# A decoder layer on one Trainium2 core: the first pass's single blocks become a pair, and the remainder block moves

## The chip, the cores and the metric

The kernel runs on one core of a Trainium2 chip. Five engines have queues of their own and work through them in order: TensorE (PE in the profile; its weight loads are shown as PEld), VectorE (DVE), ScalarE (ACT), GpSimd (POOL) and SyncE (SP), which here only issues transfers. ACT and POOL issue transfers too. 16 DMA engines move the data. The metric is the time of one execution in microseconds, the median of several runs. Everything is float32.

## The reference

One decoder layer of 16 sequences of 128 tokens and 1024 channels: self-attention, a cross-attention to a context, and a gated feed-forward layer whose weights are four-bit numbers with a scale and a zero for each group of 64.

```python
x = x + attn(layernorm(x), Wqkv, bqkv, Wo, bo)
x = x + xattn(layernorm(x), ctx, ctx, ...)
h = silu(xn @ Wg.T) * (xn @ Wu.T)
x = x + h @ Wd.T
```

Here `xn` is the normalised `x`; `Wg` and `Wu` are 2752 x 1024, `Wd` is 1024 x 2752, and each is computed from its packed numbers as `(w - zero) * scale`.

## The kernel before

**Stages.** Self-attention, cross-attention, the gate and up products of the feed-forward layer in two passes over the tokens (8 sequences each: first sequences 8 to 15, then 0 to 7), and the down products. All matrix products of the feed-forward layer are made in the manner of Strassen: seven products of half-sized operands take the place of eight, for some additions on other engines.

**Blocks.** The 2752 rows of `Wg` and `Wu` are cut into ten blocks of 256 and a remainder of 192 (`BLOCKS`, `RB = 10`). Two ways lead through them:

- `one_block` treats a single block by one level: for gate and for up seven products (`GATE`), each of four matrix multiplications with 512 columns of tokens (the tile is `p`). Each multiplication stands as two records in the profile, so a block has 112.
- `two_levels` treats pairs of blocks by two levels: seven outer products (`DOWN`, numbered 1, 2, 6, 5, 3, 7, 4), each of seven inner ones (1, 7, 6, 2, 5, 4, 3), each of four multiplications with 256 columns (the tile is `q`), 392 records a pair. GpSimd makes four left operands for each outer product (`li`, `inner_left`) from two tiles of weights (`w`), VectorE makes four right operands (`ti`, `inner_right`) in the pass's first pair. In the first pass these are stored in DRAM and loaded again for the later pairs (`again`); in the second, five of seven are kept (`KEPT`). VectorE also adds up the results (`got`, tiles `C`, `U`, `V`) and multiplies gate with up (`finish`, tile `h`).
- `last_block` treats the remainder by one level, 88 records of `p`.

The first pass takes blocks 0 and 1 one by one, then the pairs 1 to 4 (`PAIRS`, blocks 2 to 9), then the remainder. The second pass takes five pairs, then the remainder.

**Order around the change.** An engine wrapped in `InOrder` keeps the order of the program among its instructions; instructions issued without it (`nc.tensor` in block 0, `nc.gpsimd`) may be put elsewhere by the compiler. Cross-attention runs by `later(n, step)` and `tick()`: a step is run n ticks after it was noted. For each sequence VectorE and POOL divide four query tiles by their sums (`query_unit`, tile `qe`), VectorE turns them, they go out to DRAM and come back (`kd<-kt`, `qs<-kd`), and `project_out` then has four pieces (`mm<-qs,m_sb`), norms (`mm<-sq,ones`), and five steps up to `turned` and `turn_rows`, which writes the normalised rows to DRAM (`xt<-kt`). When the products of the feed-forward layer begin, the steps of the last three sequences are still to be done. They go beside block 0 and the beginning of block 1: `one_block` calls `between` after each of its 14 products, which is `beside` (L1644), and that makes one tick. From there on `moves` and `route` issue on POOL (L1133). When no step is left, `attention_done` (L1121) frees the memory of cross-attention, starts the next preparation of weights (`rest`) and opens the second set of PSUM banks.

**Preparation of weights.** `prepare` (L221) unpacks the four-bit weights on VectorE (`pa`, `pc`), stores them in DRAM (`wprep`) and is run in steps (`yield`) beside other work. The list `todo` (L324) is cut in three: `EARLY` jobs beside self-attention, those up to `MIDDLE` (18) beside cross-attention and block 0, the rest, with the first `LATE` (4) blocks of `Wd`, beside block 1 and the pairs of the first pass. The other seven blocks of `Wd` are prepared beside the second pass (`downs`, L1711). `between` in `two_levels` says how many steps go with an outer product.

**Loads of weights.** `to_load` is the list of weight tiles in order of use, `load_weights` issues the next one on SP, four tiles ahead (`AHEAD`); there are five buffers.

**Between the passes.** After the first pass's pairs, `new_blocks` and `block_loads` load the second pass's tokens (L1693 to L1697, four tiles of 1 MB, tile `b`, eight transfers). The first pass's remainder is multiplied meanwhile, and `outer_operand` forms three of four further operands from them beside it (L1662); the fourth is formed in the second pass's first pair (`last_operand`, L1479).

Of the kernel before, what the change touches and what calls it, by code (L numbers as in the profile page):

```python
# [3 lines left out]

# [78 lines left out]
def decoder_layer(  # L83
# [241 lines left out]
    EARLY, MIDDLE = 12, 18  # L325
    LATE = 4
# [265 lines left out]
    def block_loads(p, blocks, queue=nc.sync):  # L592

        for n, half in ((0, 0), (1, 0), (1, 1), (0, 1)):
            for i in range(2):
                src = xt_all[p][ds(half * BPT + 2 * i, 2), :, :, :, n]
                tc.keep_in_program_order(
                    queue.dma_start(
                        blocks[n, half][:, ts(i, TOKENS // 2)],
                        src.rearrange("b a c i j t -> (c i) (b a) j t"),  # L600
                    )
                )
                yield
# [55 lines left out]
    prep_pools(sides, "x", 2, 1)  # L659
# [18 lines left out]
    if True:  # L678
# [315 lines left out]
        for k, b in enumerate(batches):  # L994
# [15 lines left out]
            for n in (5,) if k < 12 else ():  # L1010
                later(n, lambda: next(middle, None))
# [99 lines left out]
    with ExitStack() as gs:  # L1111
# [9 lines left out]
        def attention_done():  # L1121

            nonlocal rest
            for _ in middle:
                pass
            sides.close()
            prep_pools(second, "f", 2, 2)
            rest = prepare(todo[MIDDLE:], 2, route, vector, route, loads_first=True)
            next(rest)
            banks.append(pool("c_u", 4, space=PSUM, side="right"))  # L1130
# [3 lines left out]
        flagged = []  # L1134
# [4 lines left out]
        SEQUENCE = [(mat, q) for mat in "gu" for q in GATE]  # L1139
        LAST = [("r", n) for n in range(2)] + [("m", q) for q in GATE]  # L1140

        def tiles_of(blk):
            todo = [(blk, *k) for k in (SEQUENCE if blk < RB else LAST)]
# [6 lines left out]
        PAIRS = [1, 2, 3, 4]  # L1150
        order = [blk for blk in range(RB) if blk // 2 not in PAIRS]
        order.insert(2 * PAIRS[0], None)
        to_load = deque([t for blk in order[: 2 * PAIRS[0]] for t in tiles_of(blk)])
        to_load += [t for i in PAIRS for t in tiles_of_pair(i)]
        to_load += [t for blk in order[2 * PAIRS[0] + 1 :] + [RB] for t in tiles_of(blk)]
        to_load += [t for i in range(NI) for t in tiles_of_pair(i)] + tiles_of(RB)
# [41 lines left out]
        def outer_operand(T, q):  # L1198

            b12 = blocks[0, 1]  # L1200
            if q == 7:
                vector.tensor_tensor(b12, T[3], b12, ALU.subtract)
                T[7] = b12
                return
            pool, tag = {5: (cxb, "b4"), 6: (xres, "X2"), 4: (xres, "X0")}[q]
            t = T[q] = pool.tile([P, TOKENS, JC, Q], F32, name=f"T{q}", tag=tag)
            a, b = {5: (b12, T[1]), 6: (T[3], T.get(5)), 4: (T[2], T.get(6))}[q]
# [42 lines left out]
        def one_block(blk, T, between):  # L1250

            sg = {}

            def gate(k, bank, add):
                t = sg[k] = ct.tile([P, TB], F32, name="sg", tag="sg")
                if add is None:
                    nc.scalar.activation(t, bank, AF.Silu)
                else:
                    vector.tensor_tensor(t, bank, add, ALU.add)
                    nc.scalar.activation(t, t, AF.Silu)  # L1260

            def up(k, bank, add):
                t = ch.tile([P, TB], F32, name="h", tag="h")
                if add is None:
                    vector.tensor_tensor(t, bank, sg[k], ALU.mult)
                else:
                    vector.tensor_tensor(t, bank, add, ALU.add)
                    vector.tensor_tensor(t, t, sg[k], ALU.mult)
                n, half = k
                store(blk, 1 + n, half, t)  # L1270


            engine = nc.tensor if blk == 0 else tensor
            make = {"g": products(T, gate, engine), "u": products(T, up, engine)}
            for n, (mat, q) in enumerate(SEQUENCE):
                make[mat](q)
                between(n, mat, q)

        def last_block(ps, T, between):


            PS = ps
            keys = {0: (1, 2), 1: ("e", 4)}[ps]
# [21 lines left out]
            def half_product(p, w, q, start, stop):  # L1305
                for j in range(JC):
                    tensor.matmul(
# [17 lines left out]
            between(0, "r", 0)  # L1325
# [4 lines left out]
            put_stores()  # L1330
            half_product(0, ws[0], 5, False, False)
            between(1, "r", 1)
            half_product(0, ws[1], 3, False, True)
            small(1, bank[0], bank[0])

# [24 lines left out]
            make = products(T, got)  # L1360
            for n, q in enumerate(GATE):
                make(q)
                between(2 + n, "m", q)
# [4 lines left out]
        KEPT = {1: "X8", 6: "X10", 5: "X12", 4: "X14", 7: "X4"}  # L1368
# [3 lines left out]
        class Operands:  # L1372


            def __init__(self, T, kept):
                self.T, self.kept, self.R, self.pool = T, kept, {}, None
                self.stored = {}

# [9 lines left out]
            def new(self, q):  # L1388

                tag = self.kept.get(q, "ti")  # L1390
                pool = {"ti": self.pool, "X4": xres}.get(tag, xlate)
                self.R[q] = pool.tile(
                    [P, 4, HT // Q, CHUNKS, Q],
                    F32,
                    name="ti",
                    tag=tag,
                    bufs=1 if self.kept else 3,
                )
# [61 lines left out]
        def two_levels(ps, pairs, operands, steps, between):  # L1460

            scalar = InOrder(tc, nc.scalar)
            OUTERS = [(i, q) for i in pairs for q in DOWN]
            R, place = operands.R, operands.pool
# [14 lines left out]
            def last_operand():  # L1479
                outer_operand(operands.T, 4)  # L1480
                extra.extend(operands.inner_right(4))

# [4 lines left out]
            def multiply(n, p):  # L1487
# [3 lines left out]
                if set_ == p:  # L1491
                    bank[p] = banks[n % 2].tile([P, 2, HT], F32, name=f"q{p}", tag="gu")
# [70 lines left out]
            def prepare_outer(n):  # L1563
                state[n] = {"L": {}, "bank": {}, "kept": {}}

                where = (place, "li") if ps == 0 else (ch, "h") if n == 0 else (ct, "sg")
# [7 lines left out]
            for n, (i, q) in enumerate(OUTERS):  # L1574
                last = n + 1 == len(OUTERS)
                if q in (1, 5):
                    where, name = (xres, "X6") if (ps, q) == (1, 5) else (place, "U" if q == 1 else "V")
                    sums["U" if q == 1 else "V"] = where.tile(wide, F32, name="UV", tag=name)
                load_weights()
                if n + 2 < len(OUTERS) and i > pairs[0] - (q in (7, 4)):  # L1580
# [17 lines left out]
                if ps == 1 and n == 0:  # L1598
                    extra.append(last_operand)
# [34 lines left out]

        deep = ExitStack()
# [5 lines left out]
        T1 = {}  # L1641
        first_operands, second_operands = Operands(T, {}), Operands(T1, KEPT)

        def beside(n, mat, q):  # L1644
            if rest is None:
                tick()
                if plain and not flagged and n == 5:
                    flagged.append(raise_flag())
                if not pend:
                    attention_done()  # L1650
            if blk == 2 * PAIRS[0] - 1:
                if n == 7:
                    assert rest is not None
                    route.engine = nc.sync
                    first_operands.pool = deep.enter_context(
                        tc.tile_pool(name="c_d", bufs=1, reuse_waits="tile")
                    )
                    right.extend(first_operands.inner_right(DOWN[0]))
                if n in (7, 8, 9, 11):
                    right.popleft()()  # L1660

            if blk == RB:  # L1662
                for k in {("m", 7): (5,), ("m", 6): (7,), ("m", 2): (6,)}.get((mat, q), ()):
                    outer_operand(T1, k)
                if (mat, q) == ("m", 1):
                    for step in second_operands.inner_right(1):
                        step()

            if blk == 0 and n in (2, 4, 6, 8, 10, 12):
                next(middle, None)  # L1670
            if rest is None or blk == 0 or blk == 1 and n < 4:
                return
            if blk == RB:
                steps = n < 2
            else:
                steps = n in (4, 5, 8, 10, 12)
            for _ in range(steps):
                next(rest, None)

        right = deque()  # L1680
        for blk in order:
            if blk is None:
                route.fine = True
                two_levels(
                    0,
                    PAIRS,
                    first_operands,
                    rest,
                    lambda n, i, q: {1: 2, 2: 2, 5: 2, 7: 0}.get(q, 1) if i > PAIRS[0] else 0,
                )  # L1690
                route.fine = False
                deep.close()
                cxb = pool("c_xb", 1)  # L1693
                pass1 = new_blocks(cxb, lambda k: f"b{k}")
                for _ in block_loads(1, pass1):
                    pass
                T1.update({1: pass1[0, 0], 2: pass1[1, 0], 3: pass1[1, 1]})  # L1697
                continue
            one_block(blk, T, beside)
        blk = RB  # L1700
        blocks.update(pass1)
        last_block(0, T, beside)
# [296 lines left out]
```

## Time and profile before

| | us |
|---|---|
| median of 3 runs | 2182.37 (2182.31 to 2183.66) |
| the profiled execution | 2184.46 |
| its span, first to last instruction | 2182.7 |

The stages, from the busy times by stretch (start and end in us from the span's start):

| stage | from | to | length | PE busy | DVE busy | DMA share |
|---|---|---|---|---|---|---|
| self-attention | 0.00 | 250.40 | 250.40 | 240.19 | 211.15 | 0.54 |
| cross-attention | 250.40 | 750.62 | 500.22 | 499.81 | 392.44 | 0.71 |
| block 0, end of cross-attention | 750.62 | 814.85 | 64.23 | 64.23 | 47.90 | 0.89 |
| block 1 | 814.85 | 862.91 | 48.06 | 48.06 | 25.95 | 0.67 |
| first pass, four pairs | 862.91 | 1203.04 | 340.13 | 339.42 | 239.96 | 0.72 |
| first pass, remainder | 1203.04 | 1240.81 | 37.77 | 37.77 | 22.93 | 0.97 |
| second pass, five pairs | 1240.81 | 1664.15 | 423.34 | 423.34 | 314.99 | 0.59 |
| second pass, remainder | 1664.15 | 1712.88 | 48.73 | 48.39 | 14.18 | 0.87 |
| down products | 1712.88 | 2182.70 | 469.82 | 461.80 | 232.65 | 0.72 |

PE busy is the time in which a matrix multiplication was under way; since they overlap, their spacing, a stage's length by its count, is the better price. Many instructions are recorded at L79, the helper in `InOrder`, so groups are told apart by their tiles.

### The profile page before, as it was taken

The numbers are of one execution on the slowest core, as the hardware profiler recorded it, in microseconds if no ns is written. First come the engines' busy times: TensorE is split into PE (matmuls) and PEld (weight loads), VectorE is DVE, ScalarE is ACT, GpSimd is POOL, SyncE is SP. The second block draws the span as 40 slices with busy tenths as digits, with TensorE's granted clock in tenths as the row PEclk, the third lists the DMA queues.
The fourth block names the chain that finished last, engine by engine and source line by source line (L and its number), as shares of the span: only waits on it lengthen the run. The fifth ranks groups of instructions, "written<-read, shape, count | busy, mean of one in ns | idle before, by whom it ended". The sixth has DMA issues, their size and how long they took to land.

```text
span 2182.7 us, 25252 instructions
## 1 busy us (share of the span) xinstructions
PE 2163.0 (99%) x8836; PEld 1611.3 (74%) x8836; DVE 1502.1 (69%) x2057; ACT 521.2 (24%) x704; POOL 768.7 (35%) x673
## 2 busy tenths in 40 slices
PE   8999999999999999999999999999999999999998
PEld 7565655555555555888888588888886788888887
DVE  7899578888877774777677677767765535544473
ACT  2111235655665541121122112212111000000000
POOL 5454133333343352444444244444441022323200
PEclk9999999999999999999999999999999999999999
DMA  6436447777797686577785846566657578979941
GB/s 258 150 130 223 148 152 232 226 230 234 229 293 222 191 284 225 188 269 252 268 272 195 244 150 198 201 220 229 202 185 249 188 209 228 300 178 259 269 122 59
DMA packets 266471, 467.18 MB, mean 214 GB/s; under 512 B 29504, under 2 KB 123712, under 8 KB 261344
## 3 DMA queue, kind: packets, MB, share of 16 engines
q1 hardware_dynamic: 219296, 370.04, 52.4%
q0 software_dynamic: 29312, 77.35, 13.0%
q10 hardware_dynamic: 17728, 18.09, 2.6%
q8 instruction: 72, 1.18, 0.2%
q14 instruction: 63, 0.52, 0.1%
HBM read 307.30 MB, written 157.55 MB: 213 GB/s over the span
## 4 chain that ended last, share of the span: by engine, by line
PE 95%; DVE 3%; issue 1%; DMA 1%; ACT 0%; POOL 0%; DVEq 0%; POOLq 0%
PE q L79 34%; PE po L1878 21%; PE kq L79 10%; PE mm L79 8%; PE p L79 6%; PE kx L79 5%; PE mm L435 4%; PE p L1229 2%; PE mm L450 2%; PE mm L333 1%; DVE pa L79 1%; PE tr L382 1%; DVE ti L79 0%; DVE pc L79 0%; PE mm L465 0%
## 5 line engine op out<-in xcount | busy, mean ns | idle before, releaser
L79 PE MATMUL q<-ti,li 128*128 128x256 f32 x1512 | 347.6, 379 | 0.7 <-ACT k L79 0.6
L79 PEld LDWEIGHTS q<-ti,li 128*128 128x128 f32 x1512 | 286.8, 190 | 41.3 <-ACT k L79 1.5
L79 ACT COPY k<-q 128x512 f32<-128x512 f32 x189 | 110.6, 585 | 589.9 <-PE q L79 589.8
L79 POOL TENSOR_TENSOR li<-w 128x512 f32<-128x512 f32 x126 | 173.6, 1380 | 114.8 <-DMA w<-wu 66.3
L865 POOL TENSOR_TENSOR qe<-qe,qrec 128x1024 f32<-128x1024 f32 x64 | 148.4, 2318 | 179.5 <-DVE qrec L79 142.2
L1878 PE MATMUL po<-wc,lc 128*128 128x256 f32 x840 | 184.0, 379 | 0.3 <-DVE wc L79 0.2
L1878 PEld LDWEIGHTS po<-wc,lc 128*128 128x128 f32 x840 | 159.4, 190 | 22.8 <-DVE wc L79 1.1
L79 POOL TENSOR_TENSOR li<-w,li 128x512 f32<-128x512 f32 x63 | 90.5, 1437 | 230.3 <-PE q L79 203.0
L79 DVE TENSOR_TENSOR C<-q,k 128x512 f32<-128x512 f32 x135 | 92.5, 685 | 85.0 <-PE q L79 82.1
L79 PE MATMUL q<-b,w 128*128 128x256 f32 x576 | 136.1, 379 | 0.0
L79 POOL TENSOR_TENSOR li<-li,w 128x512 f32<-128x512 f32 x63 | 84.8, 1346 | 124.5 <-PE q L79 124.3
L1878 PE MATMUL po<-wq,lq 128*128 128x256 f32 x560 | 126.7, 379 | 0.0
L79 PEld LDWEIGHTS mm<-qs,m_sb 128*128 128x128 f32 x512 | 97.3, 190 | 39.7 <-issue 28.9
L79 DVE STREAM_TRANSPOSE kt<-qe 128x1024 f32<-128x1024 f32 x64 | 79.3, 1240 | 62.0 <-POOL qe L865 57.9
L79 PE MATMUL kx<-ek,cxt 128*128 128x512 f32 x256 | 121.8, 598 | 0.0
L79 PEld LDWEIGHTS q<-b,w 128*128 128x128 f32 x576 | 109.4, 190 | 15.7 <-issue 1.0
L79 PE MATMUL mm<-qs,m_sb 128*128 128x256 f32 x512 | 120.6, 379 | 0.0
L79 PE MATMUL kq<-wq_sb,xn 128*128 128x512 f32 x256 | 120.2, 593 | 0.4 <-ACT qe L853 0.4
L79 PE MATMUL kq<-wk_sb,cx 128*128 128x512 f32 x256 | 120.1, 592 | 0.0
L79 PE MATMUL q<-ti,w 128*128 128x256 f32 x504 | 119.1, 379 | 0.0
L1878 PEld LDWEIGHTS po<-wq,lq 128*128 128x128 f32 x560 | 106.0, 190 | 15.5 <-issue 0.8
L435 PE MATMUL mm<-xnT,wqkv_sb 128*128 128x512 f32 (+1 forms) x320 | 113.3, 510 | 0.0
(205 smaller groups left out, 3777.8 us busy)
## 6 DMA issues: line engine op xcount, KB each, us to landing
w<-wu SPq DMA_DIRECT2D x140, 256.0 KB, 3.2
lq<-h SPq DMA_DIRECT2D x140, 256.0 KB, 5.1
w<-wg SPq DMA_DIRECT2D x138, 256.0 KB, 2.8
kd<-kt SPq DMA_DIRECT2D x62, 512.0 KB, 3.4
qs<-kd SPq DMA_DIRECT2D x244, 128.0 KB, 3.1
ti<-r SPq DMA_DIRECT2D x29, 1024.0 KB, 7.9
h<-h SPq DMA_DIRECT2D x80, 256.0 KB, 2.6
wq<-wd SPq DMA_DIRECT2D x70, 256.0 KB, 6.6
```

What stands on the lines that cost most here:

```text
L79: return lambda *args, **kw: self._tc.keep_in_program_order(fn(*args, **kw))
L333: tensor.matmul(ps, oT[:, d, ts(b % BPT, S)], wo_d[d][:, ts(h, 512)], start=(d == 0), stop=(d == 1),)
L382: nc.tensor.transpose(tr[:, j, :], xn[:, ts(4 * h + j, P)], ident)
L435: nc.tensor.matmul(ps[:, tokens], wqkv_sb[:, f, c, :], xnT[:, c, tokens], start=(c == 0), stop=(c == CC - 1),)
L450: nc.tensor.matmul(ps, xnT[:, c, ts(i, S)], wqkv_sb[:, 4:6, c, :], start=(c == 0), stop=(c == CC - 1),)
L865: nc.gpsimd.tensor_tensor(qe, qe, rec.unsqueeze(2).to_broadcast(wide), ALU.mult)
L1229: tensor.matmul(ps, wt[:, j, :], T[q][:, :, j], start=(first == q and j == 0), stop=(q in (2, 3, 4) and j == JC - 1), skip_group_check=True,)
L1878: nc.tensor.matmul(bank[:, i, :], l[:, ts(i, S)], w,  start=(start and c == 0 and i % 2 == 0), stop=(stop and c == len(pairs) - 1), skip_g ...
```

## The change

The first pass takes all five pairs by two levels; `one_block` is gone. The remainder of the first pass comes first, beside the end of cross-attention: its `between` is now called 11 times (four half products, seven products), makes one tick in each of the first three and two in each later one, and its multiplications go to `nc.tensor`. The preparation of the remainder's weights (`r`, `m`) is moved up to the place after the early jobs; five jobs rather than six are in the middle part, all beside cross-attention, and `LATE` is 3, so that the second pass prepares eight blocks of `Wd`. The first pass's pairs take two steps of preparation with each outer product but one, from the second pair on; the second pass's take two with all but two.

The second pass's token tiles are loaded during the last pair of the first pass, into memory that is free by then, and its first right operands are made there. The further operands (`outer_operand`) are all formed in the second pass's first pair, one of them in a tile of its own. `KEPT` names other places. In `two_levels` the sets of banks alternate across the seam.

```diff
     todo = [(blk, mat) for blk in range(RB) for mat in "gu"] + [(RB, "r"), (RB, "m")]
-    EARLY, MIDDLE = 12, 18
-    LATE = 4
+    todo[12:12] = [todo.pop(-2), todo.pop(-1)]
+    EARLY, MIDDLE = 12, 17
+    LATE = 3
...
-            for n in (5,) if k < 12 else ():
+            for n in (5,) if k < 13 else ():
                 later(n, lambda: next(middle, None))
...
-        PAIRS = [1, 2, 3, 4]
...
+        to_load = deque(tiles_of(RB))
+        to_load += [t for _ in range(2) for i in range(NI) for t in tiles_of_pair(i)] + tiles_of(RB)
...
-            pool, tag = {5: (cxb, "b4"), 6: (xres, "X2"), 4: (xres, "X0")}[q]
+            pool, tag = {5: (cxb, "b0"), 7: (cxb, "b1"), 6: (cxb, "b2"), 4: (xres, "X4")}[q]
             t = T[q] = pool.tile([P, TOKENS, JC, Q], F32, name=f"T{q}", tag=tag)
...
         def last_block(ps, T, between):
...
+            engine = nc.tensor if ps == 0 else tensor
...
-        KEPT = {1: "X8", 6: "X10", 5: "X12", 4: "X14", 7: "X4"}
+        KEPT = {1: "X12", 6: "X14", 5: "X10", 4: "X8", 7: "b3"}
...
+        for _ in middle:
+            pass
+        prep_side.close()
...
+        def beside(n):
+            for _ in range(1 if n < 3 else 2):
                 tick()
+            if plain and n == 4:
+                raise_flag()
+            if n >= 7:
+                right.popleft()()
+
         last_block(0, T, beside)
+        attention_done()
...
+        def take_block(n):
+            where = {2: (xres, "X6"), 6: (xlate, "X8"), 3: (xres, "X2"), 7: (xres, "X0")}
+            pool, tag = where[n]
+            key = AGAIN[len(pass1)]
+            pass1[key] = pool.tile([P, TOKENS, JC, Q], F32, name=f"b{key[0]}{key[1]}", tag=tag)
+            for _ in range(2):
+                next(again_loads)
+
+        def second_pass(i, q):
+            if i < NI - 1:
+                return []
+            if q in (2, 6, 3, 7):
+                take_block(q)
+            if q == 2:
+                T1[1] = pass1[0, 0]
+            return second_operands.inner_right(1) if q == 3 else []
+
+        route.fine = True
+        for step in two_levels(
+            0,
+            first_operands,
+            rest,
+            lambda n, i, q: 0 if i == 0 or q == 7 or (i, q) == (NI - 1, 3) else 2,
+            second_pass,
+        ):
+            step()
...
+        def outer_operands(i, q):
+            todo = {1: (5, 6), 2: (7,), 5: (4,)}.get(q, ()) if i == 0 else ()
+            return [lambda k=k: outer_operand(T1, k) for k in todo]
+
         remaining = two_levels(
             1,
-            range(NI),
             second_operands,
             downs,
-            lambda n, i, q: {2: 2, 5: 2, 3: 2, 7: 0}.get(q, 1) if i > 0 else 0,
+            lambda n, i, q: {6: 1, 7: 0}.get(q, 2) if i > 0 else 0,
+            outer_operands,
         )
```

## The prediction

> **What bounds the kernel now.** I read the page's busy times first, then the chain that ended last, then busy times by stretch, then the timelines of PE and POOL at the end of cross-attention.
>
> ```profile
> PE 2163.0 (99%) x8836; PEld 1611.3 (74%) x8836; DVE 1502.1 (69%) x2057; ACT 521.2 (24%) x704; POOL 768.7 (35%) x673
> ...
> PE 95%; DVE 3%; issue 1%; DMA 1%; ACT 0%; POOL 0%; DVEq 0%; POOLq 0%
> ```
>
> TensorE has work in 99% of the span and is 95% of the chain. A change pays here by taking TensorE time away, and costs where TensorE has to wait. The chain from the first pass to the down projection (start, us, what) gives a price for every stage:
>
> ```profile
> 814.85 48.07 PE p L79 x112
> 862.91 56.99 PE q L79 x264
> ...
> 943.78 259.27 PE q L79 x1200
> 1203.04 37.77 PE p L79 x88
> 1240.81 423.34 PE q L79 x1960
> ```
>
> `p` are products of 512 columns: 112 records are one block by one level, 48.07 us or 429 ns each; 88 are the remainder, 37.77. `q` are products of 256 columns: the second pass's five pairs are 1960 records in 423.34, so 392 records and 84.67 us a pair. Busy time by pair (stretch, length, then PE, PEld, DVE, ACT, POOL busy, clock, DMA share, GB/s):
>
> ```profile
> 862.91:947.60 84.69, 83.98 (x387) 72.71 (x386) 61.23 (x79) 15.85 (x25) 36.72 (x27) 1.00 0.62 220
> 947.60:1032.30 84.70, 84.70 (x394) 74.56 (x393) 57.24 (x74) 16.72 (x26) 38.76 (x28) 1.00 0.76 254
> 1032.30:1117.00 84.70, 84.70 (x395) 74.54 (x394) 59.97 (x79) 16.71 (x26) 37.77 (x28) 1.00 0.80 268
> ...
> 1579.50:1664.15 84.65, 84.65 (x393) 74.31 (x392) 64.21 (x83) 16.62 (x26) 34.73 (x25) 1.00 0.57 181
> ```
>
> Only the first pair has a hole in PE (0.71 us); a pair with VectorE at 64.21 of 84.65 has none.
>
> **One pair in place of two single blocks.** Removed: 2 x 48.07 = 96.14. Added: 84.67. That is -11.47 us on the engine that sets the end, the only gain in the change.
>
> [...]
>
> **The remainder beside the end of cross-attention.** Its 37.77 us move and cost the same; the question is the cover. From 750.62 to 814.85 TensorE did block 0 (48.07) and 16.16 us of cross-attention's last products, and block 1 followed. Now 37.77 + 16.16 = 53.93, and at 804.55 the first pair must start. The delayed steps of cross-attention come one per product for three products and then two per product (before: always one). So the last batch's four output pieces (`mm` from `qs`) stand behind the fifth product, before: two behind the sixth, two behind the seventh. PE:
>
> ```profile
> 769.56 1.88 PE L79 MATMUL mm<-sq,ones 128*128 128x512 f32 x4
> 771.28 7.03 PE L1229 MATMUL p<-T,w 128*128 128x512 f32 x16
> 778.15 3.62 PE L79 MATMUL mm<-qs,m_sb 128*128 128x256 f32 x16
> 781.60 3.60 PE L1229 MATMUL p<-b,w 128*128 128x512 f32 x8
> 785.03 3.62 PE L79 MATMUL mm<-qs,m_sb 128*128 128x256 f32 x16
> ```
>
> and POOL, which issues the loads of `qs`:
>
> ```profile
> 771.02 3.86 POOL L68 DMA_DIRECT2D qs<-kd  x7 [0.68 <-DMA w<-wu]
> 776.20 0.55 POOL L68 DMA_DIRECT2D qs<-kd  x1 [1.31 <-DMA kd<-kt]
> 778.40 2.18 POOL L68 DMA_DIRECT2D xt<-kt  x4 [1.65 <-DMA qs<-kd]
> 780.58 2.19 POOL L68 DMA_DIRECT2D qs<-kd  x4
> ```
>
> The second query's tile lands 6.9 us after its issue, 772.70 + 6.9 = 779.6, for a piece at 779.9; the fourth's lands 3.7 after 782.21, at 785.9, for a piece at 786.8. Both were just in time. In the new order TensorE is at the pieces one product (3.43) or two (6.86) earlier: second 776.4, fourth 779.9. If the loads stay, it loses 779.6 - 776.4 = 3.2, then is at the fourth at 783.1 and loses 2.8: 6.0 in all. Nothing of the change moves these loads: VectorE's and POOL's work on the queries (one TENSOR_TENSOR of 1.9 us each and its transpose) and POOL's four `xt` issues are still ahead of them. The lower bound is 0: the remainder's products are no longer held in program order with the others, so they may be put ahead of the pieces. But then VectorE is late next. Its two tests of the sums, at 789.9 and 793.8 before, stand in its queue ahead of the small product that frees the remainder's first bank. TensorE wants that bank at the eighth product: 774.7 + 6.9 (pieces) + 1.9 (norms) + 2 x 3.43 = 790.4. Without the weight preparation that VectorE did between the tests (3.3 us), the second ends at 791.7 and the bank is free at 792.5 or later: some 2 us from the other side. I take 4.5, between 0 and 6.0 and nearer to the upper row, because the order of these products before is exactly the program's.
>
> The remainder's nine weight loads and ACT's two copies go with it, and are fewer than block 0's fourteen loads in the same place. The operands of the first pair come in time in this picture: weights are loaded four tiles ahead, and the four `li` ran at 846.76 to 851.9 for a start at 862.91; VectorE's four `ti` go beside the remainder's last four products. The first pair's own loss of 0.7 to 1.2 us stays, and may grow by up to 1 with VectorE's backlog: 0.5.
>
> **Preparation of weights.** One step more (3.3 us of VectorE) goes into cross-attention, where TensorE needs 31.2 us a batch: 0. The first pass then has 5 gate/up jobs and 3 down jobs beside four pairs. A gate/up job on VectorE is two units of 2 x 0.41 + 1.22 + 1.22 and four sums of 0.68, 9.2 us; a down job is two units of 2 x 0.41 + 0.68 + 0.68 + 1.22 and two sums, 8.2. Together 70.6, or 17.7 a pair; their loads and stores go on SP's queue as before, and weight loads of the products stand behind them. What a pair needs by itself (rows `C`, `UV`, `h` of the first pass, 180.0 us over four) is 45.0. 62.7 of 84.7 is below the 64.21 that cost nothing: 0. The second pass takes an eighth down job: 8.2 / 4 = 2 us a pair more, 66.3 of 84.65: 0, and up to 1 if VectorE is then late for a bank. Without the cover of TensorE's 84.67 us a pair, these would be 70.6 and 8.2 in full.
>
> **Second pass's blocks beside the last pair.** The same eight loads of 512 KB, which took SP from 1207.23 to 1219.17 to issue and 7.4 us (median) to land:
>
> ```profile
> 1207.23 11.94 SPq L598 DMA_DIRECT2D b<-xt  x8
> ```
>
> They are now on SP in four groups between the weight and `ti` loads. Their targets were freed at least one outer product before, so SP should not wait. In 1203.04 to 1240.81 the queues moved 271 GB/s at a share of 0.97, so 4.2 MB is 15 us of all engines: 0.18 of a pair, on top of 0.80 at most. Behind them on SP stand the weight loads, and for those waits POOL, then TensorE. Weights of outer product n + 2 are loaded during n, and POOL reads them at the start of n + 1, 84.67 / 7 = 12.1 us later; they land in 3.5. A lag under some 9 us is hidden: 0, at worst 4.
>
> [...]
>
> **The seam.** The second pass now follows the first pair by pair. TensorE's banks alternate on, the first left operands and right operands are made beside the last pair. Three large subtractions (2.29 each) move from the remainder into the first pair: 64.16 + 6.9 = 71.0 of 84.7 on VectorE, denser than any row; 0 to 1.4, I take 0.5.
>
> **Sum.** -11.47 + 4.5 + 0.5 + 0.5 = -6.0. The profiled run took 2184.46, its span 2182.7, the median of the runs is 2182.37, so the span is worth the median to 0.02%: 2182.4 - 6.0 = **2176.4** (forecast, chance 0.46).
>
> **Rivals.**
> 1. Clean gain (0.20): the remainder's products fill the waits, 0 to 1.5 lost: 2171.7. For: they may be reordered. Against: VectorE's queue above.
> 2. Late loads (0.16): at the last pair the queues are full, weights or blocks come late and 4 more are lost: 2180.4, no change. For: share 0.80 before anything is added. Against: `ti` landed in 8.4 us and no product waited.
> 3. Slower (0.16): POOL's tail holds the first pair. POOL is in order, and its last `xt` issues ended at 821.17 before. If they stay there and the `li` of the first pair are queued behind them, the first is ready at 821.17 + 1.27 = 822.4 instead of 806.3, when the second inner product wants it: 16.1 lost, 2182.4 - 11.5 + 16.1 + 1 = 2188.0. It decides from 15.8 us late on. Against: the steps now come at two per product.
> 4. The change doesn't do what it says (0.02): still 3528 `q` records; 2182.
>
> About 0.2% (4.4 us) can be told from no change. Below 2178.0 lie the forecast but for a small part, and rival 1: 0.65; within, rival 2 and that part: 0.19; slower 0.16. The range runs from rival 1 without any loss to rival 2 and the beginning of rival 3: 2171 to 2184. The forecast's own: 2173 to 2179.
>
> **What would show it.** 3920 `q` and 176 `p` records; the pairs at 84.7 in both passes; PE gaps ended by DMA at `mm<-qs` about 775 to 786 (forecast), by VectorE at the remainder's eighth product (rival 1), by POOL `li` at 806 (rival 3), by loads in the last pair (rival 2). A pair above 85.5 us anywhere would make the prediction wrong.

## The result, and the profile after

The changed kernel takes 2207.32 us (median of 4 runs, 2202.57 to 2215.16) against 2183.01 for the kernel before on the same chip: a ratio of 1.0115, 95% interval 1.0083 to 1.0146. It is 1.15% slower. The profiled run took 2205.05, its span 2203.2; before, the span was 2182.7.

The page first, busy times and then the shares of the chain that ended last:

```profile
PE 2158.6 (98%) x9004; PEld 1643.9 (75%) x9004; DVE 1549.4 (70%) x2094; ACT 524.0 (24%) x709; POOL 800.4 (36%) x675
...
PE 88%; DVE 6%; DMA 3%; issue 2%; POOL 1%; ACT 1%; SPq 0%; DVEq 0%; POOLq 0%; ACTq 0%
```

TensorE's busy time fell by 4.4 us while the span grew by 20.5, and its share of the chain fell from 95% to 88%. (The busy time fell by less than the forecast's 11.47 mostly because records at half clock, shown below, count as busy.) So TensorE waits. For whom, from the feed-forward layer's first product on (749 us; engine, line, what was waited for: us in total, times, longest; the longest five):

```profile
PE q L80 <- DVE ti L80: 9.8, 4, 3.4
PE p L1222 <- DVE h L80: 7.0, 1, 7.0
PE po L1836 <- DMA lq<-h: 2.6, 1, 2.6
PE q L80 <- ACT k L80: 2.5, 3, 1.4
PE mm L80 <- DMA qs<-kd: 1.4, 1, 1.4
```

The two largest are both VectorE: one wait of 7.0 in the remainder (`p`), four of 9.8 together for right operands (`ti`). Stage by stage, taken from the first TensorE record of each stage:

| stage | before or expected, us | after, us | lost, us |
|---|---|---|---|
| remainder beside the end of cross-attention | 53.93 | 66.64 | 12.7 |
| first pair of the first pass | 86.31 | 86.70 | 0.4 |
| pairs 2 to 4 of the first pass | 84.61 | 84.61, 84.61, 84.76 | 0.1 |
| last pair of the first pass | 84.61 | 87.05 | 2.4 |
| first pair of the second pass | 84.61 | 97.80 | 13.2 |
| its other four pairs | 84.68 (mean) | 84.70 (mean) | 0.1 |
| remainder, down projection, end | 518.68 | 523.07 | 4.4 |

With 1.3 won ahead of the first product this makes 32.0, against a gain of 11.47: +20.5, the difference of the spans. 3920 `q` and 176 `p` records show that the change does what it says.

**The head.** TensorE and VectorE of the changed kernel, in order (start, length, what, and in brackets the idle time before it and what ended it):

```profile
799.53 2.82 PE L1222 MATMUL p<-T,w 128*128 128x512 f32 x6
809.41 6.64 PE L1222 MATMUL p<-b,w 128*128 128x512 f32 x8 [7.05 <-DVE h L80]
```

and VectorE in the same stretch:

```profile
802.37 1.23 DVE L80 SCALAR_TENSOR_TENSOR y<-sq,y 128x1024 f32<-128x1024 f32 x1 [5.66 <-ACT sq L939]
803.63 1.28 DVE L80 SCALAR_TENSOR_TENSOR X<-y,gs_sb,X 128x1024 f32<-128x1024 f32 x1
...
807.99 0.16 DVE L80 SCALAR_TENSOR_TENSOR shift<-mv,rstd 128x1 f32<-128x1 f32 x1 [0.67 <-POOL rstd L153]
...
808.67 0.68 DVE L80 TENSOR_TENSOR h<-p,k 128x512 f32<-128x512 f32 x1
```

The remainder's last product needs a bank that `h<-p,k` empties. Its input was done at 802.35, but the addition stood in VectorE's queue behind the last sequence's steps: `y`, itself idle for 5.66 us until ScalarE's exponential was done, then `X`, the statistics and `shift`. It ran 6.3 us late, and TensorE stood still for 7.05. The eight products that follow take 6.64 us where a row of eight took 3.60 before.

**The seam.** The last pair of the first pass and the first two of the second (stretch, length, then PE, PEld, DVE, ACT, POOL busy, clock, DMA share, GB/s):

```profile
1156.55:1243.60 87.05, 85.17 (x393) 74.18 (x392) 71.95 (x86) 16.67 (x26) 42.67 (x30) 1.00 0.86 279
1243.60:1341.40 97.80, 87.49 (x394) 75.21 (x393) 78.24 (x88) 16.69 (x26) 36.28 (x27) 0.98 0.46 145
1341.40:1426.00 84.60, 84.60 (x393) 74.44 (x392) 62.00 (x84) 16.69 (x26) 40.99 (x28) 1.00 0.66 218
```

The same pair in the kernel before, the first of the second pass:

```profile
1240.81:1325.48 84.67, 84.67 (x394) 74.51 (x394) 64.15 (x80) 16.39 (x27) 36.84 (x27) 1.00 0.45 156
```

VectorE around the second of the waits:

```profile
1268.83 2.28 DVE L80 TENSOR_TENSOR T<-b,b 128x2048 f32<-128x2048 f32 x1
1271.03 0.68 DVE L80 TENSOR_TENSOR C<-q,k 128x512 f32<-128x512 f32 x1
1271.74 1.74 DVE L80 TENSOR_TENSOR C<-C,UV 128x512 f32<-128x512 f32 x1
1273.40 1.75 DVE L80 TENSOR_TENSOR ti<-T 128x512 f32<-128x512 f32 x1
1275.18 0.69 DVE L80 TENSOR_TENSOR ti<-T,ti 128x512 f32<-128x512 f32 x1
```

and TensorE there:

```profile
1271.36 1.89 PE L80 MATMUL q<-ti,li 128*128 128x256 f32 x8
1276.02 3.62 PE L80 MATMUL q<-ti,li 128*128 128x256 f32 x8 [2.78 <-DVE ti L80]
```

VectorE does 78.24 us of work in the second pass's first pair, against 62.00 in the next and 64.15 in the same pair before. It is in no pair full, yet TensorE waits: the `ti` that a product needs at 1273.2 comes fourth behind a subtraction of 2.28. Of the four waits (0.84, 2.78, 2.78 and 3.38 us) the first three stand behind such a subtraction; the last, at 1332.69, has none in its outer product, but right operands among VectorE's additions.

In the last pair of the first pass the longest wait, 1.4 us, is one for ScalarE's `k`, and it comes before any right operand is made there (1217 us). From the chain that ended last:

```profile
1178.96 1.68 DVE pa L80
1180.66 2.18 DVE pa L80
...
1184.45 1.77 DVE pc L80
...
1189.16 33.15 PE q L80 x152
```

These are steps of the preparation of weights. The sum `C` stands behind them on VectorE, ScalarE waits 2.61 us for `C`, and its copy of `k`, which TensorE needs, stands behind that.

### The profile page after: what moved, and what is told of

It reads as the page before. It is cut to its first block, busy times and chain, and to the rows that moved or that the text cites. A ratio compares the mean times of both kernels' runs of the same rounds, so it can differ in the third digit from the quotient of the medians.

```text
span 2203.2 us, 25710 instructions
## 1 busy us (share of the span) xinstructions
PE 2158.6 (98%) x9004; PEld 1643.9 (75%) x9004; DVE 1549.4 (70%) x2094; ACT 524.0 (24%) x709; POOL 800.4 (36%) x675
## 4 chain that ended last, share of the span: by engine, by line
PE 88%; DVE 6%; DMA 3%; issue 2%; POOL 1%; ACT 1%; SPq 0%; DVEq 0%; POOLq 0%; ACTq 0%
PE q L80 35%; PE po L1836 19%; PE kq L80 10%; PE mm L80 8%; PE kx L80 5%; PE mm L437 4%; PE mm L452 2%; DMA wq<-wd 2%; PE p L80 2%; PE mm L335 1%; DVE pa L80 1%; DVE C L80 1%; DVE ti L80 1%; PE p L1222 1%; PE p L1272 1%
## 5 line engine op out<-in xcount | busy, mean ns | idle before, releaser
L80 PE MATMUL q<-ti,li 128*128 128x256 f32 x1680 | 389.4, 381 | 12.5 <-DVE ti L80 9.8
L80 PEld LDWEIGHTS q<-ti,li 128*128 128x128 f32 x1680 | 318.9, 191 | 60.5 <-issue 12.2
L80 ACT COPY k<-q 128x512 f32<-128x512 f32 x210 | 122.5, 584 | 649.0 <-PE q L80 649.0
L80 POOL TENSOR_TENSOR li<-w 128x512 f32<-128x512 f32 x140 | 192.5, 1379 | 85.8 <-PE q L80 61.0
L80 POOL TENSOR_TENSOR li<-w,li 128x512 f32<-128x512 f32 x70 | 111.3, 1590 | 247.8 <-PE q L80 229.8
L80 DVE TENSOR_TENSOR C<-q,k 128x512 f32<-128x512 f32 x150 | 102.8, 685 | 87.6 <-PE q L80 84.8
L80 POOL TENSOR_TENSOR li<-li,w 128x512 f32<-128x512 f32 x70 | 96.0, 1371 | 123.5 <-PE q L80 122.7
L80 PE MATMUL q<-T,w 128*128 128x256 f32 x560 | 132.4, 379 | 0.0
L80 PE MATMUL q<-ti,w 128*128 128x256 f32 x560 | 132.3, 379 | 0.0
L80 DVE TENSOR_TENSOR C<-C,UV 128x512 f32<-128x512 f32 x120 | 114.9, 958 | 4.1
```

The costliest lines, as they stand in the source:

```text
L80: return lambda *args, **kw: self._tc.keep_in_program_order(fn(*args, **kw))
```

## The experiments

Each is an edit of the changed kernel. "Head" is the stretch with the remainder; "seam" is the second pass's first pair. Stretches are from one profiled run each, and the clock alone moves them: four kernels with the seam's VectorE work unchanged have the same four waits to 0.01 us and seams of 96.12, 97.80, 99.33 and 99.48, as half clock follows none, one, two and two of the waits, at 1.5 to 1.8 us each. Differences of the seam below that are said to be without the half clock have this taken off.

**The head: who holds it.** The first kernel spreads cross-attention's delayed steps, one for each product throughout:

```diff
-            for _ in range(1 if n < 3 else 2):
-                tick()
+            tick()
```

> The remainder at the head of the first pass makes one tick after each of its 11 products instead of one and then two; the steps of cross-attention left over run after the last product. Theory (VectorE's queue): the steps of the last sequence (y, X, row statistics) stood ahead of the remainder's own additions on VectorE and waited there for ScalarE, so TensorE sat 7.05 us before its last product and then ran 3.3 us at half clock; moved behind, from 749.3 to the first product of a pair should take 55 to 59 us instead of 66.6, and the time fall by 7 to 11 us. Rival (GpSimd's queue): the first pair is held by its left operands, which stand behind the last transfers of cross-attention; these now come later, so a wait on li of 5 us or more appears at the second inner product and the time falls by less than 4 us. Rival (loads of qs, as forecast): the waits at the pieces are what counts, and since the pieces come one or two products later the wait of 1.6 us goes, and no more than 3 us with it.

Measured: 2206.89 us, ratio to before 1.0106 (1.0086 to 1.0125); the head falls to 54.57, as VectorE's theory has it, but the first pair grows from 86.70 to 100.17, and the time doesn't move. The wait has gone to GpSimd, on whose queue the first pair's left operands (`li`) stand behind the last sequence's `x_all`, `rstd` and `xt`:

```profile
789.15 2.18 POOL L69 DMA_DIRECT2D xt<-kt  x4 [4.18 <-DVE kt L80]
807.46 0.56 POOL L901 DMA_DIRECT2D x_all<-X  x1 [16.12 <-DVE X L80]
809.48 0.55 POOL L153 TENSOR_TENSOR rstd<-rstd,mhalf 128x1 f32<-128x1 f32 x1 [1.46 <-DVE rstd L80]
813.37 2.22 POOL L69 DMA_DIRECT2D xt<-kt  x4 [3.34 <-DVE kt L80]
815.61 2.49 POOL L80 TENSOR_TENSOR li<-w 128x512 f32<-128x512 f32 x2
```

GpSimd idles 16.12 us with `li` behind it; TensorE's waits in that stretch are nearly all this one:

```profile
PE q L80 <- POOL li L80: 10.6, 1, 10.6
```

The next kernel therefore also makes the first four left operands ahead of the last steps:

```diff
...
         last_block(0, T, beside)
+        first_left = {}
+        first_comb = inner_left(first_left, ch, "h")
+        for k in (7, 5, 6, 3):
+            first_comb(k)
         attention_done()
```

> One tick per product, and GpSimd makes the first pair's four left operands before the steps of cross-attention that are left over. Theory (two queues hold the tail in turn: VectorE's additions, then GpSimd's left operands behind rstd and xt): the wait of 10.8 us for li and the half clock after it go; the stage of the remainder stays at 54 to 56 us, the first pair falls from 100.2 to 85 to 89, and the time by 10 to 14 us against one tick per product, to 2189 to 2197. Rival: the tail of cross-attention holds the pair in any case (its memory, its banks, VectorE's steps); then another wait of 5 us or more takes the place of li and the first pair stays above 93.

Measured: 2198.85 us (1.0064, 1.0047 to 1.0081); head 54.60, first pair 92.55, above the 85 to 89 expected. Of the excess over 86.31, 6.2 are left, a wait of 4.3 and half a clock behind it. The profile names no engine for this wait:

```profile
PE q L80 <- issue: 4.3, 1, 4.3
```

ScalarE may be next; its queue in the kernel that has this edit and the seam's below:

```profile
810.45 1.53 ACT L169 ACTIVATE xn<-X,shift,rstd 128x512 f32<-128x512 f32 x2 [5.03 <-DVE shift L80]
811.89 1.05 ACT L80 COPY k<-q 128x512 f32<-128x512 f32 x2
```

The copies of `k`, which empty TensorE's banks, stand behind two normalisations that wait 5.03 us for VectorE's `shift`. To test this, the normalisations of the last sequence go to VectorE, which waits for the same `rstd` anyway.

> e7_both with one step more changed: the two normalisations of the last sequence's rows are done by VectorE, which waits for the same rstd anyway, instead of by ScalarE. Nothing is left out. Three queues theory: what is left of the hole at the first pair (4.3 us at 812.55, and some 2 us of product records at double spacing behind it) is ScalarE's copy of k, queued behind the two normalisations that wait for VectorE's shift. With them off ScalarE the first pair falls from 92.56 to 86.5, and the time by some 6 us, to 2188.5. Rival, the chain itself: the wait goes to whatever stands behind the next link (VectorE's ti or C sums behind the normalisations it now waits in): the first pair stays above 90 and the time at 2193 to 2196. The second pass's first pair isn't touched: 93 to 98 by both.

Measured: 2195.00 us (1.0057, 1.0040 to 1.0074); first pair 92.55, unchanged. That decided nothing: the edit took sequence 15, and cross-attention ends with sequence 7. The same on the right one:

```diff
-                normalise_act(dst, rows, b)
+                if b == batches[-1]:
+                    vector.tensor_scalar(
+                        dst, rows, mv[:, b, 0:1], rstd[:, b : b + 1], ALU.subtract, ALU.mult
+                    )
+                else:
+                    normalise_act(dst, rows, b)
```

> What e8_norm_dve was meant to be: there the edit fell on sequence 15, the last by number, while cross-attention ends with sequence 7, whose normalisations stayed on ScalarE (810.66 and 811.39, with the copies of k at 812.10 and 812.57 behind them). Here it falls on the one that ends last. Nothing is left out. Three queues theory: the hole of 4.3 us at 812.5 and the product records at double spacing behind it (some 1.7) go, the first pair falls from 92.55 to 86.5, the time to 2188 to 2190. Rival, the chain itself: the wait goes to what stands behind the next link; the first pair stays above 90 and the time at 2193 to 2196.

Measured: 2189.25 us (7 runs; 1.0035, 1.0024 to 1.0046). The head is 54.57 and the first pair 86.31, exactly that of the kernel before. ScalarE's queue now has no normalisation ahead of the copies:

```profile
803.95 0.60 ACT L1327 ACTIVATE sg<-p 128x512 f32<-128x512 f32 x1 [1.10 <-PE p L1229]
805.68 0.59 ACT L80 COPY k<-q 128x512 f32<-128x512 f32 x1 [1.13 <-PE q L80]
```

So the loss at the head is three in-order queues, VectorE, GpSimd and ScalarE, each with a link of the last sequence's serial chain in it and the products' work behind that link. Freed in this order, each hands the wait to the next; all three freed, head and first pair take 140.88 us in place of 153.34.

**The seam: loads, right operands or subtractions.** Three single changes: the big subtractions left out; three of the four blocks' loads left out; the right operands of outer product 4 made earlier, in outer product 3.

```diff
         def outer_operand(T, q):
 
-            b12 = blocks[0, 1]
+            T[q] = T[{5: 1, 7: 2, 6: 3, 4: 3}[q]]
+            return
```

> The second pass's four further operands (subtractions of 128 x 2048 on VectorE in its first pair) are left out; the loaded tiles stand in for them. Theory (VectorE at the seam): these 9.1 us of VectorE, in bursts of 2.28 ahead of the additions and right operands that TensorE needs, cause the waits at 1260.9, 1276.0 and 1304.9; without them the first pair of the second pass takes 85 to 89 us instead of 93.2 and the time falls by 6 to 10 us; the wait at 1332.7, in an outer product without such a subtraction, stays. Rival (late loads): the seam waits for the blocks or weights that were loaded beside the last pair; nothing changes by more than 2 us.

```diff
             key = AGAIN[len(pass1)]
+            if pass1:
+                pass1[key] = pass1[0, 0]
+                return
```

> Only the first of the second pass's four blocks is loaded beside the last pair; it stands in for the other three, so 3 MB in six transfers are left out. Theory (VectorE at the seam): the second pass's first pair stays at 92 to 94 us, at most the 2.9 us lost in the last pair of the first pass go; time falls by 0 to 4 us. Rival (late loads): the last pair and the seam lose 13 us because the queues are full; the time falls by 8 us or more.

```diff
                 extra.extend(more(i, q))
+                if (ps, i, q) == (1, 0, 3):
+                    extra.extend(operands.inner_right(4))
```

> In the second pass's first pair the four right operands of the last outer product are formed one outer product earlier (in the extra places of outer product 3 instead of beside outer product 7, where VectorE has three additions for each result). Theory: the 3.5 us wait at 1332.7 is VectorE having 2.7 us of right operands in its fullest outer product; it goes, and the time falls by 2 to 4 us. Rival: the wait is VectorE's backlog from the four large subtractions and only moves; change under 1 us.

Measured (time, ratio and its interval, last pair, seam; the changed kernel has 87.05 and 97.80):

| left out or moved | us | ratio | last pair | seam |
|---|---|---|---|---|
| subtractions | 2197.21 | 1.0058 (1.0041 to 1.0075) | 86.72 | 90.69 |
| 3 MB of block loads | 2203.12 | 1.0098 (1.0081 to 1.0115) | 86.97 | 96.12 |
| right operands of 4 | 2202.12 | 1.0085 (1.0069 to 1.0102) | 87.10 | 96.06 |

Without three quarters of the loads the last pair is as long as with them, and the seam has the very waits of the changed kernel; its 1.7 less is the half clock that did not come. The loads aren't what either waits for. The subtractions are 7.1 of the 13.2: without them only the wait of 3.38 is left of the four. Moving the one set of right operands takes just that wait away, but smaller ones for ScalarE grow, and 1.7 is what remains.

Next, bursts or sum? The subtractions cut in halves and spread over four outer products, with the right operands of 4 spread too; then this together with the edit that makes the left operands first:

```diff
-            vector.tensor_tensor(t, a, b, ALU.subtract)
+            vector.tensor_tensor(t[:, rows], a[:, rows], b[:, rows], ALU.subtract)
...
-            todo = {1: (5, 6), 2: (7,), 5: (4,)}.get(q, ()) if i == 0 else ()
-            return [lambda k=k: outer_operand(T1, k) for k in todo]
+            todo = {1: (5, 6), 2: (4,), 6: (7,)}.get(q, ()) if i == 0 else ()
+            steps = [lambda k=k, h=h: outer_operand(T1, k, h) for k in todo for h in range(2)]
+            if i == 0 and q in (5, 3):
...
+                steps.extend(last_right.popleft() for _ in range(2))
+            return steps
```

> The changed kernel with only the second pass's first pair rearranged: the four large subtractions in halves, in outer products 1 (two), 6 and 2 (one each), and the last outer product's right operands in the places of 5 and 3 instead of beside 7. The same work on VectorE. Theory (bursts on VectorE, not its sum): the second pass's first pair falls from 97.8 to 87 to 92, the time by 5 to 9 us, to 2196 to 2201. Rival (VectorE's sum, 74.9 of 84.6 with its waits): the waits only move, the pair stays above 94. The tail at the head of the first pass stays as in the changed kernel, 66 us.

> Both edits together. Theory: the gains add, since they are 400 us apart: head 54 to 56, first pair 85 to 89, second pass's first pair 87 to 92, time 2180 to 2190, within 0.4% of the kernel before. If the down projection's waits of 0 to 4.5 us are tied to the delays ahead of them they go too, and the time is 2176 to 2182, faster than before.

Measured: 2201.71 us (1.0079, 1.0062 to 1.0096) with a seam of 96.43, and 2194.42 (1.0046, 1.0029 to 1.0063) with 94.75. Without the half clock (once in the changed kernel, twice and once here) that is 92.9 and 93.0 against 96.0: smaller pieces bring 3 us, and two waits of 2.75 stay, at other products. The pair stays above 94, as the rival said; the burst is the smaller part.

Two more, built on the kernel with the mistaken normalisation: all of the seam's big subtractions on GpSimd, and, as a bound on what any place for them can bring, none. There are four of them (the one for outer product 4 stood in this pair before the change too), where the expectation counts the three that moved.

```diff
-            vector.tensor_tensor(t[:, rows], a[:, rows], b[:, rows], ALU.subtract)
+            nc.gpsimd.tensor_tensor(t[:, rows], a[:, rows], b[:, rows], ALU.subtract)
```

> e8_norm_dve with the three big subtractions of the seam (in halves, as there) done by GpSimd instead of VectorE. Nothing is left out. VectorE's sum theory: the second pass's first pair is longer than 84.6 because VectorE has more than it can do between the products that wait for it; without these 6.9 us it falls to 87 to 89, and the time by 6 to 7 us against e8_norm_dve. Rival, GpSimd next: its subtractions take two to three times VectorE's time and stand ahead of its li in the same queue, so TensorE waits for li in place of ti and the pair stays at 93 or more; the time is within 2 us of e8_norm_dve, or above it.

> e8_norm_dve without the three big subtractions of the seam: loaded tiles stand in for their results, so this work is left out. It bounds what any other place for them can bring. VectorE's sum theory: the second pass's first pair falls to 85 to 88, the time to some 7 to 9 us below e8_norm_dve, 2180 to 2182, no lower than before by more than 3. If the pair stays above 91, the subtractions are not what it lacks and the right operands of outer product 4 alone (or the reuse of a buffer) are.

Measured: on GpSimd 2195.56 us (1.0051, 1.0034 to 1.0068), the same as on VectorE; left out 2187.35 (10 runs; 1.0017, 1.0007 to 1.0027), 7.65 less. Last pair and seam by stretch, with the subtractions on GpSimd:

```profile
1151.55:1242.88 91.33, 86.86 (x394) 75.54 (x392) 77.88 (x86) 16.71 (x26) 50.94 (x33) 0.97 0.81 267
1242.88:1333.64 90.76, 86.38 (x393) 74.74 (x392) 74.64 (x85) 16.72 (x26) 51.03 (x32) 0.99 0.47 155
```

and with the subtractions left out:

```profile
1150.57:1237.07 86.50, 85.11 (x394) 74.30 (x393) 73.29 (x86) 16.68 (x26) 43.37 (x29) 1.00 0.87 281
1237.07:1324.20 87.13, 85.31 (x393) 74.23 (x392) 65.90 (x85) 16.70 (x26) 37.22 (x27) 1.00 0.49 163
```

On GpSimd the seam falls by 4.2 (from 94.91) and the last pair grows by 4.7 (from 86.59): GpSimd takes the first subtractions up early, two halves of them in the last pair (1231.26 and 1235.25). VectorE, which does none of them, is busy 77.88 us there in 86 operations, where the run without subtractions has 73.29 in as many: beside them two `h<-C` take 4.52 us, and TensorE waits 3.7 us for a `C` behind them, with half clock after it. Left out, VectorE's work in the seam is 65.90 and TensorE loses 2.5. So VectorE's work between products that wait for it sets this pair, within 2.5 us.

The last kernel keeps all corrections and puts only the subtractions for outer products 7 and 4 on GpSimd:

```diff
-            vector.tensor_tensor(t[:, rows], a[:, rows], b[:, rows], ALU.subtract)
+            engine = nc.gpsimd if q in (7, 4) else vector
+            engine.tensor_tensor(t[:, rows], a[:, rows], b[:, rows], ALU.subtract)
```

> e11_norm_last with two of the seam's three big subtractions later in the pair (the operands of outer products 7 and 4, in halves) on GpSimd, the earlier ones (5 and 6) left on VectorE. Nothing is left out. VectorE's sum theory: the second pass's first pair falls from 94.9 to 90 or below as in e9_T_pool (90.76), and the last pair of the first pass stays at 86.6, since the work that made it 91.33 there (the first operands, on GpSimd beside it) is back on VectorE: 4 us less than e11_norm_last, 2184 to 2186. Rival, GpSimd next: li queued behind them; the pair stays at 93 or more and the time within 2 us of e11_norm_last.

Measured: 2187.72 us (8 runs; 1.0023, 1.0012 to 1.0034). The last pair is 85.62, the seam 93.39, 4.1 less together than without the move (86.71 and 96.43), of which 2.4 are left without the half clock. The median falls by 1.5 only, and the intervals overlap: the gain isn't shown, and the rival (GpSimd next) fits. Half a subtraction takes GpSimd 2.36 to 3.81 us here, VectorE 1.2. The wait for `ti` is joined by one for GpSimd:

```profile
PE q L80 <- DVE ti L80: 2.8, 1, 2.8
...
PE q L80 <- POOL li L80: 2.1, 1, 2.1
```

No version beats the kernel before. Nor would these edits by much if the subtractions cost nothing: the median without them, 2187.35, less the 6.2 us that the right normalisation took off the first pair, makes an estimate of 2181, 0.1% below the 2183.84 of the kernel before on the same chip, and the ten runs behind it spread over 8.5 us.

## Why the prediction was wrong

It said 2176.4, faster; it was 2207.32.

- **One pair for two blocks, -11.47:** right. The added pair costs 84.61, and its 392 `q` records stand 216 ns apart as before (84.67). Per column that is, to 1%, what a single block's records of 512 columns take (429 ns), and the weight loads run underneath: from 904.30 to 989.00 PEld is busy 74.56 us and PE all 84.70.
- **Waits for `qs` at cross-attention's end, +4.5 (0 to 6.0):** the failing step at the head. The remainder's first products are put between the pieces, at 749 to 767 us, and those waits are 1.4 for `qs` and 0.5 for ScalarE (0.8 to 3.0 for `qs` in the other four profiled runs with this head; the 3.0 had half clock behind it and cost 3.1 more). What the prediction called VectorE late next, some 2 us, was 7.05 and then 3.0 of half clock. It asked when VectorE would finish two tests that it saw in the row of before; it did not follow the last sequence's chain (pieces, norms, exponential, `y`, `X`, statistics, `rstd`, `shift`, normalisation, transpose, `xt`) link by link and ask on each engine what stands behind the link. Before, block 1's products of 48.07 us lay over that chain; the change takes this cover away, and the prediction compared the weight loads of the two places but put no price on the lost cover.
- **Rival 3, GpSimd's tail:** the right mechanism in second place. With VectorE out of the way it cost 10.6, then half clock; the prediction gave it 16.1. In the changed kernel itself VectorE's wait hides it.
- **First pair, +0.5:** 0.4 over the kernel before; 0.6 to 1.8 in the other four profiled runs with this head, with waits of up to 0.9 for `li`, so the hit is partly luck.
- **Preparation, 0:** right in pairs 2 to 4 of the first pass and the second pass's others, which take 84.6 to 84.8; not in the last pair.
- **Blocks beside the last pair, 0 (up to 4):** the loads cost nothing measurable there, as predicted; the pair still lost 2.4, 1.4 of it in the wait behind the preparation's additions and 0.5 in one for VectorE's `C`. VectorE is busy 71.95 us there, where the prediction summed 62.7 for a pair; the next pass's right operands are 3.4 of that, and additions such as `pa` and `pc` above took 1.7 to 2.2 us beside GpSimd where the sum had 0.7 to 1.2.
- **The seam, +0.5 (0 to 1.4):** the second failing step, 13.2. The sum of 71.0 was called denser than any row, and then priced as if it were one: the bound of 1.4 came from no row of the profile. VectorE's busy time was 78.24, not 71.0, mostly because its additions lengthen beside GpSimd (below), and the right question was not the share but the order: three of the four subtractions stand ahead of a `ti` that a product waits for, and the right operands of outer product 4 are late without one.
- **Remainder, down projection and end, not priced:** 4.4. From the remainder's first product to the first down product it is 0.85 more in every kernel with the change (38.62 against 37.77; in the changed kernel that product waits 0.7 for ScalarE's `sg`), the end is 1.3 to 2.2 longer, and the down projection varies.

"A pair above 85.5 us anywhere would make the prediction wrong" was a good mark, if a careless one: the first pair of the kernel before has 86.31.

Open: the down projection takes 472.16 to 473.05 in the profiled runs of seven kernels with the change and 474.4 to 478.8 in six, against 472.93 before. The loss stands always some 207 us after its start, at one product that waits for `lq` or `u`; in the chain of the changed kernel three loads `wq<-wd` of 8.7 to 15.4 us lie ahead of it. The DMA engines are full around that place in the kernel before too (share 1.01 in 52 us, 0.96 after). Why some executions lose it, and why the changed kernel spreads over 13 us where that of before spreads over 2, wasn't tried; its four runs had mean granted clocks of 0.997, 0.996, 0.994 and 0.993, from the fastest to the slowest.

## What to carry to other kernels

Long work at a seam is cover: before it is replaced by something shorter, list the serial chain that ran beneath it, and for each link ask what is queued behind it on its own engine, for every engine, since freeing one queue only showed the next here (waits of 7.05, 10.6 and 4.3 us in turn). VectorE was busy only 78.24 of 97.80 us at the seam, and yet TensorE waited 9.8 us there for its `ti`: price added work by the order of the engine's queue at the product that waits, and a sum denser than any row of the profile has no bound from the profile. Take a load's or an operation's duration from rows in which the same neighbours run: VectorE's additions took 0.69 us alone and 1.16 on the mean beside GpSimd's `li`.

## What the runs showed of the hardware

**The clock after a wait.** In these runs TensorE's clock was granted at half after some of its waits, those of 2.78, 4.3, 7.05 and 10.6 us below among them. Stretches of the changed kernel (the clock is the number before the DMA share):

```profile
803.00:808.00 5.00, 0.00 (x0) 0.00 (x0) 4.19 (x9) 1.27 (x2) 1.11 (x2) 0.71 0.82 243
808.00:813.00 5.00, 3.59 (x5) 1.53 (x6) 4.54 (x8) 1.57 (x2) 0.00 (x0) 0.50 0.48 148
813.00:818.00 5.00, 5.00 (x15) 3.06 (x14) 1.71 (x2) 0.79 (x2) 4.75 (x7) 0.76 0.72 173
```

After the wait of 7.05 us the products stand 0.85 us apart, not 0.43, until 815.5: 6 us at half, 3.0 lost on top. After the 10.6 us of the first experiment it is 6.1 us and 3.1 lost; after the second of the seam's waits, 2.78 us, a row of eight products takes 3.62 us instead of 1.89, while those of 2.78 and 3.38 later in the same pair passed without (clock 1.00 from 1300 to 1310 and from 1328 to 1341). In the trace's record of the granted clock these stretches at half are 10.24 us (from 805.12, within the wait) and 3.41 us (from 1276.16). In the first experiment the clocks of the 5 us from 808, 813, 818 and 823 are 0.64, 0.50, 0.50 and 1.00, some 13.6 us at half, an estimate from these four; around the wait of 4.3 us in the kernel that makes the left operands first they are 0.95 from 808 and 0.71 from 813, some 3.4 us by the same sum. So a wait of TensorE can cost more than its length, here by 1.5 to 3.1 us where the clock falls. The length of the wait alone doesn't say whether it falls: one of 2.78 us had half clock behind it, one of 3.38 had not, and what else decides it wasn't shown.

**VectorE beside GpSimd.** VectorE's additions of 128x512 with both inputs in SBUF (`C<-C,UV`, `ti<-b,ti`, `h<-h,sg` and the like) take 0.69 us where no `li` of GpSimd overlaps them (200 in the changed kernel from 749 to 1720 us, none above 0.70) and 1.16 on the mean, up to 1.81, where one does (189); those with one input in PSUM (`C<-q,k`) take 0.68 in both cases (157 and 132). Beside the rows of 1.74 and 1.75 at 1271.74 and 1273.40 shown above, GpSimd ran these:

```profile
1271.67 1.27 POOL L80 TENSOR_TENSOR li<-w,li 128x512 f32<-128x512 f32 x1 [3.91 <-PE q L80]
1273.33 1.27 POOL L80 TENSOR_TENSOR li<-w 128x512 f32<-128x512 f32 x1 [0.40 <-PE q L80]
```

In the seam the time above 0.69 adds up to 13.54 us, in the same pair before to 8.19: the difference is 5.4 of the 7.2 by which VectorE's 78.24 us exceed the 71.0 of the prediction.
